# Splitting the levels of a WKV recurrence by feature halves and placing one batch's levels between the other's outputs

## The chip, the cores and the metric

The kernel runs on one core of one Trainium2 chip. The metric is the device time of one execution in microseconds; a smaller one is better. The kernel is one program that holds a whole small network (two layers of conditioning, token mixing, routing, attention and feed-forward). The change touches one stage of it, the recurrence of the first token mixer.

## The reference, cut to what matters

The stage computes the recurrence of an RWKV-6 mixer. For each of 2 batches there are 1024 tokens and 256 features in 4 heads of 64. `r`, `k`, `v` are projections of the tokens, `w` a decay between 0 and 1 for each token and feature, `u` a bonus for the token itself.

```
def step(S, inputs):                      # S: 64 x 64 for each head
    rt, kt, vt, wt = inputs
    kv = kt[..., :, None] * vt[..., None, :]
    y = jnp.einsum('bhi,bhij->bhj', rt, S + u[None, :, :, None] * kv)
    S = wt[..., :, None] * S + kv
    return (S, y)
...
mean = y.mean(-1, keepdims=True)
var = y.var(-1, keepdims=True)
yn = ((y - mean) * jax.lax.rsqrt(var + LN_EPS)).reshape(b, t, c)
yn = yn * ln_w + ln_b
return yn @ W_o
```

The result is added to the residual `x`. What follows (`cond2_0`, a gelu projection) needs the finished `x`.

## The kernel before, in words

Features lie on the partitions: 256 features are two halves `c` of 128 partitions, and each half holds two heads (`par`, 64 partitions each). `r[b]`, `kk[b]`, `w[b]` are tiles of 128 x 2 x 1024 for each batch `b`. Tokens are cut into 8 chunks (`ck`) of 128, and each chunk into two halves of 64.

The function `wkv` (line 399) never steps through tokens. It builds the triangular matrix A of all pairs (earlier token, later token) inside a chunk by levels:

- `diagonal` (427) makes the products of a token with itself, from `ru` = u times r (line 581, ScalarE), and places them on A's diagonal (443, VectorE).
- `level` (445) for l = 0 to 5, with h = 2^l: 64 matmuls of 64x64 by 64x32 for each batch and level (line 455) make the products of pairs that fall on two sides of a boundary of blocks of h tokens. They go to two PSUM banks, one for each `par`; both feature halves `c` lie in each bank. A matmul in fp32 leaves two records, so the profile counts 128 for a batch and level. VectorE copies the wanted entries to A under a mask for l up to 3 (468, two copies of 128x512), ScalarE for l = 4 and 5 (475, small blocks).
- `decay` (477) after each level multiplies k by the total decay behind it (483, GpSimd, 128x1024) and r by that before it (484, VectorE, 128x1024), in place, so that the next level can use them; line 486 then halves the table of total decays `tot`.
- `last` (489) makes the products between the two halves of a chunk (495, 64 records a batch), copied by ScalarE and VectorE (503), and a last decay.

Then `states` (506) transposes k (513, TensorE; 516, ScalarE copies to `kt`), makes each chunk's contribution to the state (530, copied to `pd` by 537) and runs a scan over the chunks (540, VectorE). `output` (543) makes two chunks of y at a time: products with A (552) and with the state (563) in two banks, which 574 (ScalarE) and 575 (VectorE) add into `y`. `tmix_out` (610) normalises 512 tokens and projects them: squares (618, ScalarE), sums (623), root (180 to 182), widened (628), transposed (634), multiplied (637, 638), and projected by `wo` (643) onto `x` (644).

The order of the work is set by the program text and by a planner that merges the engines' queues by its own cost table; the order of each queue is then fixed. Before the change the two batches alternate: for each level, batch 0's and then batch 1's (lines 583 to 586), with four banks named `sc` shared in turn. After both have passed all levels, `states` of both follow, then the four `output` steps of batch 0 and the four of batch 1, and between these the pieces of `tmix_out` for the 512-token chunks that are ready (lines 594 to 607). Tiles of the level part (`ru`, the tables `tot`) and of the output part (`kt`, `td`, `pd`, `st`) lie in two pools, one opened after the other.

SP's queue issues the loads of the next stage: `b2` (949), `c2w1`, `c2w2` and their small companions (134 to 144), then `w1c` (1068) and the first expert's weights (933, 935). Each waits until the memory that it is to fill is free, and each stands behind the ones before it.

Of the kernel before, what the change touches and what calls it, by code (L numbers as in the profile page):

```python
# [9 lines left out]
F32 = mybir.dt.float32  # L10
# [3 lines left out]
ALU = mybir.AluOpType  # L14
# [5 lines left out]
B = 2  # L20
# [378 lines left out]
def wkv(k, r, kk, w, v, y, x):  # L399

# [6 lines left out]
    with (  # L411
        tiles(tc, name="wka", bufs=1) as ap,
        tiles(tc, name="wkq", bufs=1, space=PSUM) as qp,
    ):
# [3 lines left out]

        A = [ap.tile([P, 2, 2, NC, P], F32, name=f"A{b}") for b in range(B)]
        tot = [w[b].rearrange("p c t -> p (c t)") for b in range(B)]  # L420
# [3 lines left out]
        def bank(pp, shape):  # L424
            return pp.tile(shape, F32, name="sc", bufs=4)

        def diagonal(pp, b, ru):

            for c in range(2):
                ps = [bank(pp, [P, NC, H]) for par in range(2)]  # L430
                for ck in range(NC):
                    for half in range(2):
                        ts = slice(ck * P + half * H, ck * P + (half + 1) * H)
                        for par in range(2):
                            nc.tensor.matmul(
                                ps[par][halves[half], ck, :],
                                lhsT=kk[b][halves[par], c, ts],
                                rhs=ru[halves[par], c, ts],
                                start=True,
                                stop=True,  # L440
                            )
                for par in range(2):
                    nc.vector.tensor_mul(A[b][:, par, c, :, 0:H], ps[par], eye.unsqueeze(1).to_broadcast([P, NC, H]))

        def level(pp, b, l):

            h = 1 << l
            ps = [bank(pp, [P, 2, NC, H // 2]) for par in range(2)]
            for c in range(2):
                for ck in range(NC):  # L450
                    for half in range(2):
                        ts = slice(ck * P + half * H, ck * P + (half + 1) * H)
                        for par in range(2):
                            rv = r[b][halves[par], c, ts].rearrange("p (n two h) -> p n two h", two=2, h=h)
                            nc.tensor.matmul(
                                ps[par][halves[half], c, ck, :],
                                lhsT=kk[b][halves[par], c, ts],
                                rhs=rv[:, :, 1, :],
                                start=True,
                                stop=True,  # L460
                            )
            for par in range(2):
                dv = A[b][:, par, :, :, 0:H].rearrange("p c n t -> p (c n) t")
                dv = dv.rearrange("p g (n two h) -> p g n two h", two=2, h=h)[:, :, :, 1, :]
                pv = ps[par].rearrange("p c n t -> p (c n) t").rearrange("p g (n h) -> p g n h", h=h)
                if h < 16:
                    m = k.lvl[:, l].rearrange("p g (n h) -> p g n h", h=h)
                    nc.vector.copy_predicated(dv, m, pv)
                    continue

                for s0 in range(0, P, 32):
                    n = (s0 % H) // (2 * h)
                    if s0 % (2 * h) < h:
                        ss = slice(s0, s0 + min(h, 32))
                        nc.scalar.copy(dv[ss, :, n, :], pv[ss, :, n, :])

        def decay(sp, b, l):
            h = 1 << l
            n = 2 * S // (2 * h)
            t2 = tot[b].rearrange("p (n two) -> p n two", two=2)  # L480
            kv = kk[b].rearrange("p c (n two h) -> p (c n) two h", two=2, h=h)
            rv = r[b].rearrange("p c (n two h) -> p (c n) two h", two=2, h=h)
            nc.gpsimd.tensor_mul(kv[:, :, 0, :], kv[:, :, 0, :], t2[:, :, 1].unsqueeze(2).to_broadcast([P, n, h]))
            nc.vector.tensor_mul(rv[:, :, 1, :], rv[:, :, 1, :], t2[:, :, 0].unsqueeze(2).to_broadcast([P, n, h]))
            nt = sp.tile([P, n], F32, name=f"tot{l}", bufs=2)
            nc.vector.tensor_mul(nt, t2[:, :, 0], t2[:, :, 1])
            tot[b] = nt

        def last(pp, b):

            for c in range(2):
                ps = [bank(pp, [P, NC, H]) for par in range(2)]
                for ck in range(NC):
                    for par in range(2):
                        nc.tensor.matmul(
                            ps[par][halves[0], ck, :],
                            lhsT=kk[b][halves[par], c, ck * P : ck * P + H],
                            rhs=r[b][halves[par], c, ck * P + H : (ck + 1) * P],
                            start=True,
                            stop=True,  # L500
                        )
                for par, copy in enumerate((nc.scalar.copy, nc.vector.tensor_copy)):
                    copy(A[b][halves[0], par, c, :, H:P], ps[par][halves[0]])
            decay(ap, b, 6)

        def states(sp, b):
            kt = sp.tile([P, NC, C], F32, name="kt", bufs=1)
            for n in range(0, M, 2):
# [7 lines left out]
                nc.scalar.copy(kt[:, n:e, :], pk[:, 0 : e - n, :])  # L516

            td = sp.tile([P, 2, H, M], F32, name="td")
# [5 lines left out]
            pd = sp.tile([P, 2, H, M], F32, name="pd", bufs=1)  # L524
# [13 lines left out]
            st = sp.tile([P, 2, H, M], F32, name="st")  # L538
            flat = [t.rearrange("p c j n -> p (c j n)") for t in (st, td, pd)]
            nc.vector.tensor_tensor_scan(flat[0], flat[1], flat[2], 0.0, ALU.mult, ALU.add)  # L540
            return st

        def output(sp, b, st, n):

            py = [qp.tile([P, 2, 2, 2, H], F32, name=f"py{half}") for half in range(2)]
            for c in range(2):
                for i in range(2):
# [12 lines left out]
                    for own in range(2 if ck else 0):  # L560
                        for half, hs in enumerate(halves):
# [3 lines left out]
                                lhsT=st[hs, c, :, ck - 1],  # L565
# [4 lines left out]
                            )  # L570
            yv = y[:, :, b * S + n * P : b * S + (n + 2) * P].rearrange("p c (i a t) -> p c i a t", i=2, a=2)
            for a in range(2):
                t = sp.tile([P, 2, 2, H], F32, name="half")
                nc.scalar.copy(t, py[0][:, :, :, a])
                nc.vector.tensor_add(yv[:, :, :, a], t, py[1][:, :, :, 1 - a])

        with tiles(tc, name="wks", bufs=2) as sp, tiles(tc, name="wkp", bufs=1, space=PSUM) as pp:
            for b in range(B):
                ru = sp.tile([P, 2, S], F32, name="ru")
                for c in range(2):  # L580
                    nc.scalar.activation(ru[:, c, :], r[b][:, c, :], AF.Copy, scale=k.vec("u", c))
                diagonal(pp, b, ru)
            for l in range(6):
                for b in range(B):
                    level(pp, b, l)
                    decay(sp, b, l)
            for b in range(B):
                last(pp, b)
        with (
            tiles(tc, name="wkt", bufs=2) as sp,  # L590
            tiles(tc, name="gos", bufs=1) as gs,
            tiles(tc, name="gop", bufs=1, space=PSUM) as gp,
        ):
            outs = [tmix_out(k, gs, gp, y, x, ch) for ch in range(NCK)]
            before = [states(sp, b) for b in range(B)]
            left = []
            for b in range(B):
                for n in range(0, NC, 2):
                    output(sp, b, before[b], n)
                    for _ in range(2):  # L600
                        if left and next(left[0], 1):
                            left.pop(0)
                    if n % 4 == 2:
                        left.append(outs[(b * S + n * P) // CK])
            for steps in left:
                for _ in steps:
                    pass


def tmix_out(k, sp, pp, y, x, ch):  # L610

# [28 lines left out]
    for c in range(2):  # L640
        po = pp.tile([P, CK], F32, name="pw", bufs=2)
# [976 lines left out]
def attn1_heads(k, b, x, ci, kT, v, sv, masks, rp, sp, pp, yp):  # L1618
# [22 lines left out]
    def behind(ins, other):  # L1641

        how = mybir.DependencyInfo(mybir.DependencyClass.NoSync, mybir.DependencyReason.DATA)
        k.tc.add_manual_dep(ins.ins, other.ins.name, how, reason="order")

# [75 lines left out]
    def exps(it, pair):  # L1721

        for view in window(it["at"][0]):
# [5 lines left out]
            if pair and it["no"]:  # L1729
                behind(e, rows["turned"])  # L1730
# [8 lines left out]
    def invert(it):  # L1739

        rd = sp.tile([P, 4], F32, name="rd")
        behind(nc.vector.reciprocal(rd, it["den"]), rows["least"])
        it["rdw"] = sp.tile([P, 4, 64], F32, name="rdw")
        behind(nc.scalar.copy(it["rdw"], rd.unsqueeze(2).to_broadcast([P, 4, 64])), rows["exp"])

    def turn(it):
# [25 lines left out]
        behind(masked, rows["least"])  # L1772
# [352 lines left out]
```

## Time and profile before

| what | value |
|---|---|
| median of 3 runs | 1491.24 us (1489.38 to 1491.75) |
| the profiled execution, its own time | 1490.23 us |
| its span in the profile | 1488.5 us (so 1.7 us lie around the span) |
| TensorE / VectorE / ScalarE / GpSimd busy over the span | 94% / 59% / 44% / 15% |
| last projection of the stage ahead ends, about | 132.5 us from the span's start |
| first diagonal matmul (435) | 134.21 us |
| first level matmul (455) to last (455) | 139.7 to 186.0 us |
| first transpose of the states (513) | 194.29 us |
| first matmul of the next stage, `cond2_0` (671) | 271.33 us |

So the stage takes the stretch from about 134 to 271 us, a tenth of the span. The profile's page gives averages over the whole span; what counts here is read from this stretch, with the view that gives each engine's busy time by stretches, and the view of instructions in order of time. In the first, each row has the stretch, its length, for each engine the busy time and the number of instructions (x), the clock granted to TensorE as a share of full speed, the share of the DMA engines and what they moved. In the second, a row has the start, the time, the engine, the line, operation and operands, the number of instructions merged, and in brackets how long the engine had been idle and what released it.

### The profile page before, as it was taken

Reading aid. Unit: us, or ns where it says so; the run is one execution under the profiler, and the core shown is the slowest. Engines: PE = TensorE matmul, PEld = TensorE weight load, DVE = VectorE, ACT = ScalarE, POOL = GpSimd, SP = SyncE. Lnnn points to the kernel's source line nnn. Section 1 sums busy time; section 2 is a strip of 40 time slices with the busy share of each in tenths; the row PEclk is TensorE's granted clock in tenths of the full one; section 3 lists DMA queues with packets and bytes.
Section 4 is the critical chain, followed back from the end, with each engine's and each line's share of the span. In section 5 each row is a group of like instructions: output and inputs, shape, how many; then the busy total and the mean of one; then the engine's idle time right before and its main releaser. Section 6 shows DMA issues by size and latency. Waiting matters only on the chain. (4 is left out here: it accounts for less than half of the span.)

```text
span 1488.5 us, 27374 instructions
## 1 busy us (share of the span) xinstructions
PE 1405.7 (94%) x10852; PEld 930.2 (62%) x10852; DVE 874.3 (59%) x2640; ACT 651.8 (44%) x1509; POOL 217.9 (15%) x201
## 2 busy tenths in 40 slices
PE   6998889999799999979999999999999999999998
PEld 3445877455556676656666644777776457777766
DVE  5545734121389942047787773577676637777674
ACT  3333242222222213207788832656564436556633
POOL 3333630022401632110000010000000200000011
PEclk9899678999889999989999999999999999999999
DMA  9600004300144343030000020000000000000001
GB/s 300 203 1 2 4 2 142 142 31 30 64 133 160 106 147 121 15 127 1 2 1 2 2 85 0 1 2 2 1 2 2 0 0 2 2 2 2 1 15 45
DMA packets 42759, 70.79 MB, mean 48 GB/s; under 512 B 7168, under 2 KB 35840, under 8 KB 39552
## 3 DMA queue, kind: packets, MB, share of 16 engines
q1 hardware_dynamic: 36576, 57.12, 11.4%
q0 software_dynamic: 3072, 8.65, 1.6%
q10 hardware_dynamic: 2976, 3.18, 0.7%
q8 instruction: 88, 1.44, 0.4%
q14 instruction: 47, 0.39, 0.1%
HBM read 45.09 MB, written 23.86 MB: 46 GB/s over the span
## 5 line engine op out<-in xcount | busy, mean ns | idle before, releaser
L1726 ACT ACTIVATE pe<-pe,nm 128x321 f32<-128x321 f32 x256 | 142.2, 559 | 109.2 <-DVE nm L1707 109.2
L1707 DVE CUSTOM_DVE_ANT_0 pe<-ps,wbs 128x321 f32<-128x321 f32 x256 | 114.8, 491 | 18.3 <-PE ps L1680 8.3
L1255 ACT ACTIVATE pe<-pe,nm 128x256 f32<-128x256 f32 x256 | 110.5, 498 | 19.6 <-DVE nm L1245 19.6
L988 PE MATMUL ph<-xt,w 128*128 128x512 f32 x256 | 114.3, 604 | 2.2 <-ACT xt L983 2.2
L996 PE MATMUL po<-w,h 128*128 128x256 f32 x512 | 111.8, 379 | 0.0
L996 PEld LDWEIGHTS po<-w,h 128*128 128x128 f32 x512 | 97.3, 190 | 16.6 <-issue 3.8
L1245 DVE CUSTOM_DVE_ANT_0 pe<-ps,lc 128x256 f32<-128x256 f32 x256 | 94.1, 417 | 19.1 <-PE ps L1229 18.2
L1680 PE MATMUL ps<-kT,qT 64*64 64x386 f32 (+3 forms) x1024 | 101.6, 490 | 3.2 <-ACT qT L1660 2.5
L918 DVE SCALAR_TENSOR_TENSOR lc<-iok,idx,lc 128x256 f32<-128x256 f32 x248 | 100.6, 500 | 0.0
L1810 PE MATMUL py<-ptt,v 128*64 128x128 f32 x1408 | 91.0, 277 | 0.0
L1000 POOL DMA_INDIRECT ys<-ye,row x32 | 63.0, 1970 | 180.4 <-DVE ye L999 160.7
L988 PEld LDWEIGHTS ph<-xt,w 128*128 128x128 f32 x256 | 48.6, 193 | 62.5 <-issue 55.9
L1810 PEld LDWEIGHTS py<-ptt,v 128*64 128x64 f32 x1408 | 75.5, 137 | 10.7 <-issue 10.7
L1757 PE MATMUL pt<-ident,pe 128*128 128x128 f32 x512 | 77.4, 280 | 0.0
L1264 PE MATMUL ptp<-ident,pe 128*128 128x128 f32 x512 | 73.0, 280 | 3.7 <-DVE pt L1268 3.0
L1264 PEld LDWEIGHTS ptp<-ident,pe 128*128 128x128 f32 x512 | 55.3, 141 | 30.9 <-ACT pe L1255 14.8
L991 ACT ACTIVATE h<-ph,vecs 128x512 f32<-128x512 f32 x64 | 44.0, 687 | 69.5 <-PE ph L988 69.5
L1757 PEld LDWEIGHTS pt<-ident,pe 128*128 128x128 f32 x512 | 56.8, 141 | 12.5 <-issue 10.0
L999 DVE TENSOR_TENSOR ye<-po,b 128x256 f32<-128x256 f32 x32 | 13.9, 434 | 79.2 <-PE po L996 79.2
L1680 PEld LDWEIGHTS ps<-kT,qT 64*64 64x64 f32 x1024 | 33.3, 132 | 42.1 <-issue 24.4
L1765 DVE TENSOR_TENSOR ptt<-pt,near 128x1024 f32<-128x1024 f32 x48 | 58.6, 1220 | 0.4 <-PE pt L1757 0.4
L671 PE MATMUL ph<-x,c2w 128*128 128x512 f32 (+2 forms) x160 | 58.4, 508 | 0.0
(365 smaller groups left out, 2674.3 us busy)
## 6 DMA issues: line engine op xcount, KB each, us to landing
w<-in_mw SPq DMA_DIRECT2D x16, 1024.0 KB, 5.0
xs<-z SPq DMA_DIRECT2D x8, 1088.0 KB, 12.0
ys<-z SPq DMA_DIRECT2D x4, 1024.0 KB, 11.3
xe<-xs SPq DMA_DIRECT2D x7, 544.0 KB, 7.2
more<-xs SPq DMA_DIRECT2D x7, 544.0 KB, 4.1
out_x<-o SPq DMA_DIRECT2D x8, 256.0 KB, 2.2
x<-in_xT SPq DMA_DIRECT2D x3, 512.0 KB, 6.3
wa<-in_wa SPq DMA_DIRECT2D x1, 1536.0 KB, 8.0
```

What stands on the lines that cost most here:

```text
L918: nc.vector.scalar_tensor_tensor(n, key, k.idx[:, qb, j : j + 1], n, ALU.is_equal, ALU.add)
L988: nc.tensor.matmul(ph, lhsT=w1[:, c, m * P : (m + 1) * P], rhs=xt[:, c, :], start=c == 0, stop=c == 1)
L996: nc.tensor.matmul(po, lhsT=h[:, m, j * P : (j + 1) * P], rhs=w2[:, m, :], start=m == 0, stop=m == 7)
L1000: nc.gpsimd.indirect_dma_start(out=rows[e * 4 + j], out_offset=bass.IndirectOffsetOnAxis(ap=row[:, j : j + 1], axis=0), in_=ye[:, j, :], i ...
L1245: nc.vector.tensor_tensor_reduce(out=pe[:, j, :], in0=it["ps"][i][:, j, :], in1=k.lc[:, q0 + j, :], scale=-1.0, scalar=3.0e38, op0=ALU.add ...
L1255: nc.scalar.activation(pe[:, j, :], pe[:, j, :], AF.Exp, bias=nm, scale=-1.0)
L1264: nc.tensor.transpose(ptp[:, kb, j, :], it["pe"][i][:, j, kb * P : (kb + 1) * P], k.ident)
L1680: nc.tensor.matmul(ps[hps[half], view.head, c0:c1], lhsT=rows["qT", n // 2, m // 4][hp, (m + pair) % 4, qs], rhs=kT[hp, m + pair, view.sta ...
L1707: rows["least"] = nc.vector.tensor_tensor_reduce(out=pe[:, j], in0=ps[:, i, view.used : view.used + W], in1=wbs[:, o : o + W], scale=-1.0, ...
L1726: e = nc.scalar.activation(part, part, AF.Exp, bias=it["nm"][:, col], scale=-1.0, accum_out=it["den"][:, col])
L1757: nc.tensor.transpose(to[:, 2 * pair + view.head, :], pe[:, at : at + P], k.ident)
L1810: nc.tensor.matmul(py[64 * i : 64 * i + 64, (m + pair) % 4, :], lhsT=keys[j][:, hs], rhs=it["pt"][:, j, 2 * pair + i, :], start=False, sto ...
```

## The change

- `level`, `decay` and `last` become one generator, `levels(b)`, that works by feature halves. For each level and each half c: 32 matmuls, then `decay(b, l, c)` on 128x512 (GpSimd and VectorE), then the copies of that half to A (VectorE 128x256, or ScalarE with half as long blocks). A manual order puts VectorE's copies behind its own decay. After the second half comes `total(b, l)`.
- The two banks of a level are still one for each `par` and hold both halves.
- Batch 0's levels run alone, with three pairs of banks in turn (`sc`, `py`, `pk`/`pu`). Batch 1's have the pair `sc` alone; one half level is taken at each step of batch 0's `states` and `output`, so they stand between the instructions of these.
- `states` of batch 1 comes after that, then the outputs of batch 1.
- Memory: `ru` is written into `y`, the tables `tot` into w and one tile T for each batch, `kt` and the states into w, `td` and `pd` into k. The pools of the output part are gone, and all is open from the start. The projections of `tmix_out` go to the banks `pk` and `pu`, which `states` uses too.

The core of the diff:

```
+        turns = [("sc0", "sc1"), ("py0", "py1"), ("pk", "pu")]
+        def banks(shape):
+            turns.append(turns.pop(0))
+            return [qp.tile(shape, F32, name=n) for n in turns[-1]]
...
+        def decay(b, l, c):
             h = 1 << l
+            n = S // (2 * h)
+            t2 = tot[b].rearrange("p (c n two) -> p c n two", c=2, two=2)[:, c]
+            kv = kk[b][:, c].rearrange("p (n two h) -> p n two h", two=2, h=h)
+            rv = r[b][:, c].rearrange("p (n two h) -> p n two h", two=2, h=h)
+            nc.gpsimd.tensor_mul(kv[:, :, 0, :], kv[:, :, 0, :], t2[:, :, 1].unsqueeze(2).to_broadcast([P, n, h]))
+            return nc.vector.tensor_mul(
+                rv[:, :, 1, :], rv[:, :, 1, :], t2[:, :, 0].unsqueeze(2).to_broadcast([P, n, h])
+            )
...
+        def levels(b):
+            for l in range(6):
+                h = 1 << l
+                ps = banks([P, 2, NC, H // 2])
+                for c in range(2):
+                    for ck in range(NC):
+                        for half in range(2):
...
+                    scaled = decay(b, l, c)
+                    for par in range(2):
+                        dv = A[b][:, par, c, :, 0:H]
...
+                        if h < 16:
+                            m = k.lvl[:, l, 0:NC].rearrange("p g (n h) -> p g n h", h=h)
+                            behind(k, nc.vector.copy_predicated(dv, m, pv), scaled)
+                            continue
...
+                                nc.scalar.copy(dv[ss, :, n, :], pv[ss, :, n, :])
+                    if c:
+                        total(b, l)
+                    yield
...
+        for b in range(B):
+            diagonal(b)
+        for _ in levels(0):
+            pass
+        turns[:] = [("sc0", "sc1")]
+        beside = levels(1)
+        for _ in outputs(0):
+            next(beside, None)
+        for _ in beside:
+            pass
+        for _ in outputs(1):
+            pass
...
-        po = pp.tile([P, CK], F32, name="pw", bufs=2)
+    for c, name in enumerate(("pk", "pu")):
+        po = pp.tile([P, CK], F32, name=name)
```

`outputs(b)` is a new generator: `states(b)` (which now yields after each transposed pair of chunks and after each half of the contributions), then the four `output` steps, each with a yield in its middle and at its end, and after each up to two pieces of `tmix_out`.

In the built program every other stage has the same instructions in the same order on all five queues; one load, `w1ak` (1513), moves from the end of the row of loads to its front.

## The prediction

> **What bounds the stage now.** The page's chain of work that ended last says nothing here: followed back, it ends in the attention. So I read the stretch from 134 to 271 us in two views. First, busy time by stretches: diagonal, levels 0 to 3, levels 4 and 5, `last`, states, outputs, and the last chunk's tail up to the next stage's first matmul (271.33).
>
> ```profile
> 134.20:140.20 6.00, 5.16 (x258) 4.64 (x258) 4.77 (x15) 3.08 (x3) 0.00 (x0) 1.00 0.01 3
> 140.20:174.90 34.70, 28.09 (x1160) 27.26 (x1163) 30.85 (x27) 0.00 (x0) 19.14 (x8) 0.69 0.02 4
> 174.90:186.20 11.30, 9.13 (x390) 8.77 (x384) 3.68 (x3) 8.10 (x20) 8.81 (x3) 0.73 0.02 5
> 186.20:194.30 8.10, 6.88 (x131) 6.42 (x127) 4.47 (x6) 4.47 (x8) 6.46 (x3) 0.60 0.02 4
> 194.30:212.40 18.10, 15.53 (x192) 11.36 (x192) 5.99 (x7) 6.55 (x14) 4.93 (x3) 0.78 0.00 1
> 212.40:259.90 47.50, 46.72 (x532) 37.23 (x530) 18.23 (x37) 15.08 (x29) 2.86 (x12) 0.83 0.33 107
> 259.90:271.30 11.40, 9.03 (x33) 5.52 (x32) 3.76 (x6) 3.00 (x4) 0.00 (x0) 0.70 0.62 243
> ```
>
> The reader is to see that levels 0 to 3 are VectorE's (third engine column: 30.85 of 34.70 us, with 27 instructions that follow each other), that the outputs are TensorE's (46.72 of 47.50), and that VectorE has 29 us free in the outputs. That is what the change is after: VectorE's work of one batch beside TensorE's work of the other.
>
> Second, the order in time, for the prices:
>
> ```profile
> 140.26 2.06 PE L455 MATMUL sc<-r,k 64*64 64x32 f32 x125 [0.30 <-DVE A L443]
> 142.36 2.51 DVE L468 COPY_PREDICATED A<-lvls,sc 128x512 f32<-128x512 uint8 x2 [0.96 <-PE sc L455]
> ...
> 158.95 1.32 DVE L468 COPY_PREDICATED A<-lvls,sc 128x512 f32<-128x512 uint8 x2 [0.21 <-PE sc L455]
> 159.26 2.11 POOL L483 TENSOR_TENSOR k<-k,tot 128x1024 f32<-128x1024 f32 x1 [1.61 <-PE sc L455]
> 160.18 2.28 DVE L484 TENSOR_TENSOR r<-r,tot 128x1024 f32<-128x1024 f32 x1
> ...
> 175.00 1.23 DVE L484 TENSOR_TENSOR r<-r,tot 128x1024 f32<-128x1024 f32 x1 [1.02 <-PE sc L455]
> 175.10 2.95 POOL L483 TENSOR_TENSOR k<-k,tot 128x1024 f32<-128x1024 f32 x1 [2.20 <-PE sc L455]
> ```
>
> A decay of r that starts before GpSimd's takes 1.23 us and GpSimd's then 2.95; one that starts later takes 2.28. One waits for the other. And TensorE's clock:
>
> ```profile
> 151.00:154.00 3.00, 2.96 (x111) 2.86 (x106) 2.95 (x4) 0.00 (x0) 2.41 (x1) 0.50 0.02 5
> 166.00:169.00 3.00, 2.18 (x128) 2.07 (x127) 2.48 (x4) 0.00 (x0) 2.03 (x1) 1.00 0.03 5
> ```
>
> At the granted clock 0.50 a level's record takes 2.96/111 = 26.7 ns, at 1.00 2.18/128 = 17.0 ns. A half level has 64 records: 1.71 or 1.09 us.
>
> **The wait that the halves bring.** Both halves lie in the same two banks. In the built program the second half's matmuls wait for VectorE's (ScalarE's, at l = 4 and 5) copies of the first half: 18 of the 64 records for the first copy, 46 for the second. So within a level nothing of the second half runs beside the copies of the first; what TensorE does run ahead is the next level's first half, in another pair of banks. Batch 1 has one pair alone, so there every half level waits for the copies of the one before it. The handover from copy to copy is: 0.05 us from VectorE to TensorE (the copy before the 140.26 row ended at 140.2), 46 records (1.23 us at clock 0.50, 0.78 at 1.00), and 0.2 us to VectorE's start (diagonal: started at 134.21, 64th record at 135.25, VectorE at 135.43). That is 1.5 or 1.0 us. I take 1.5: in 147 to 164 us the clock stood at 0.50, and there a level's 128 records came every 3.7 us; the new stage brings fewer (below).
> The Trainium skill speaks against this sharing: "PSUM — Partial Sum Buffer", section "PSUM bank collisions raise a hardware error", says to guard the PSUM by bank and 32-partition quadrant, not by address, so halves in one bank cannot overlap on two engines. No row here shows a matmul into a bank that is being read; by addresses alone the sum would be that of the third rival.
>
> **Part 1: batch 0's levels alone.** VectorE's prices for a half: decay 0.68 (the table's halving of 128x512, line 486, took 0.684); two copies 2 x 0.65 at l = 0 and 1 (half of 2.51, with a little start-up), 2 x 0.38 at l = 2 and 3 (half of 1.32). Unknown is what GpSimd's half decay costs VectorE: nothing if VectorE is first, half of 2.28 - 1.23 = 0.5 if last; I take 0.5 for the first halves at l = 2 and 3, where the row shows it, and keep 0 and 0.5 everywhere as ends.
> - Start: VectorE is free of the diagonal at 140.9 (before, 141.4: the halvings of `tot` that stood between its copies move into the handovers, which hide them: 0.68, 0.42 and 0.28 us in the first).
> - l = 0, 1: 2 x (2 x (0.68 + 1.3) + 1.5) = 10.9. l = 2, 3: 2 x (2 x (0.68 + 0.76) + 0.5 + 1.5) = 9.8. To 161.6.
> - l = 4, 5: ScalarE's copies took 0.361 (256 elements) and 0.576 (512), so 0.25 for 128: 8 a half, 2.0, then 4 x 0.36 = 1.45. 2 x 2.0 + 1.3 + 2 x 1.45 + 1.3 = 9.5, pick-up 0.5. To 171.6.
> - `last`: 92 records took 5.19 us at clock 0.5, so 32 take 1.8; then GpSimd's half decay, 3.46/2 = 1.7. The states' transposes can begin at 171.6 + 1.8 + 0.2 + 1.7 = **175.3**. Before, at 194.29. Gain 19.0 us: batch 1's levels are gone from here, but batch 0's take 34 us alone where both took 54.
>
> **Part 2: batch 1's levels between batch 0's states and outputs.** Twelve half levels in series: 4 x (1.5 + 1.98) = 13.9; 4 x (1.5 + 1.44) = 11.8; 2 x (1.3 + 2.0) = 6.6; 2 x (1.3 + 1.45) = 5.5; the two groups of `last` with their copies (0.58) 2 x 2.1 = 4.2. Sum 42.0. What the states and outputs put into these queues: on VectorE the scan (2.03, half of it beside a group's matmuls: 1.0), the copy to `td` (0.85) and y's adds (0.42 each), mostly in handovers: 0.8. On TensorE about 8 instructions stand between two half levels; 128 records of an output step took 3.25 us (216.62 to 219.86), so 0.4 us, hidden beside copies of 0.76 to 1.3 us. Together 43.8: to **219.1**. Done by then: batch 0's states, three of its four outputs, and the sums (623) of chunk 0.
>
> **Part 3: the rest.** Before, seven outputs and `tmix_out` of chunks 0 to 2 took 47.5 us. Now: two outputs fewer (3.55 and 3.25 us in the trace, so -6.8), chunk 0's sums gone (-1.95), batch 1's states more (transposes 5.7 and contributions 6.8 us of TensorE for both batches, so +6.25), and 0.5 for their banks, shared with the projection (643), whose add (644, 0.69) must read them first. 45.5: to 264.6. The tail of the last chunk stays, 11.4: **276.0**, against 271.3.
>
> The loads do not stand in the way. `c2w1` was issued at 226.90; now it waits for batch 1's scan, by the sum near 243, and lands in 6.4 us, needed at 276. `c2w2` of batch 1 waits for the last output, some 15 us ahead of the next stage, as `w1c` did (256.37); it is used only with that stage's third chunk. The loads behind them on SP's queue, the experts', were issued at 257 to 272 and are first used at 415.6. If this cover were gone, a load costs its 5 to 7 us. `ru` in `y`'s place costs nothing: what read that memory was the zero fill, whose traffic ended by 74 us (the page's GB/s row); nor does `w1ak`, issued behind that fill into an idle queue.
>
> **Sum.** +4.7 us on the profiled execution, 1490.23: 1494.9. The median shown is 1.0 above it; I write **1495**. A difference under 0.2% (3 us) cannot be told from none.
>
> **Rivals.**
> 1. The clock stays up (ends faster). All 18 handovers were priced at clock 0.50, six in part 1 and twelve in part 2, and so were the four groups of `last`. At 1.00: 18 x 0.45 + 4 x 0.55 = -10.3, so 1484.5. For it: each queue of matmuls is short of 2 us of pause, and at 164 and 181 us the clock came back with VectorE still the pace. Against: it fell at 147 after one pause of 1.7 us and stayed down 17 us though TensorE is recorded busy 2.96 of 3.00. It decides from a mean clock of about 0.8 between 141 and 219 us: above that the change is no longer slower.
>    The Trainium skill, "TensorE: Matmul & The Clock Gate", section "HAM oscillation — how this bites in real kernels", gives the rule that only idle gaps over about 3.4 us lower the clock; by it the sum would be this rival's. The trace's fall after 1.7 us differs.
> 2. The fill holds up the levels (slower still). TensorE's queue is in order: where an output or state instruction between two half levels waits itself (for `kt`'s copy, 0.59, or the two of y's half, 0.65), batch 1's next group stands behind it. At 0.6 us for each of 13 gaps, +7.8: 1503. For it: in 194 to 212 the transposes waited 2.5 us in all for `kt`. Against: most gaps hold products with A, which wait for nothing.
> 3. The halves overlap after all, and the handovers of the second halves are hidden: 12 x 1.5 = -18, 1477. The built program's waits speak against it.
> That the change doesn't reorder as said is out: the built order shows batch 1's half levels between batch 0's instructions.
>
> **Chances.** Forecast 0.50 (its own range 1491 to 1500: GpSimd's 0.5 us at 0 and everywhere is -1 and +4), rival 1 0.27, rival 2 0.18, rival 3 0.05. Range 1482 to 1505: it takes in rivals 1 and 2 and leaves out the third and the outer ends. Faster by over 0.2% (under 1488.3): most of rival 1 (0.23) and rival 3, 0.28. Within: the rest of rival 1 and the low end of the forecast (0.14), 0.18. Slower (over 1494.2): 0.54.
>
> **What would show it.** In the profile after: the first transpose of the states near 175; VectorE idle some 1.5 us before each second half's decay, released by TensorE; batch 1's last level group near 217; 45 us from there to the last chunk's sums; the clock near 0.5 to 0.7 in the levels. The prediction is wrong in part 1 if VectorE shows no such pauses, in part 2 if the twelve half levels take under 36 or over 50 us, in part 3 if the next stage starts more than 60 us after the last of them, or waits for a load.

## The result, and the profile after

The changed kernel takes **1515.9 us** (median of 5 runs, 1513.7 to 1518.1) against 1489.4 us before (5 runs beside them, 1488.4 to 1491.8): ratio 1.0173, 95% interval 1.0159 to 1.0188. It is slower, as forecast, but by 26.5 us and not by 5: outside the range. The profiled execution took 1515.1 us, its span is 1513.3.

The change renumbers lines: level matmul 455 -> 488; VectorE's copy 468 -> 502, ScalarE's 475 -> 509; decay 483 -> 463 (GpSimd) and 484 -> 464 (VectorE); halving 486 -> 474; last 495 -> 517; transposes 513 -> 540; outputs 552 and 563 -> 579 and 590; sums 623 -> 650.

First, busy time by stretches of the changed kernel: levels 0 to 3 of batch 0, its levels 4 and 5, its last group, batch 1's levels between states and outputs, the rest, the tail. The columns are those of the first table of the prediction.

```profile
137.50:164.60 27.10, 17.75 (x521) 17.12 (x514) 15.99 (x30) 0.04 (x1) 12.42 (x8) 0.55 0.01 3
164.60:176.70 12.10, 9.65 (x226) 9.39 (x226) 2.97 (x5) 7.14 (x25) 6.35 (x5) 0.50 0.01 3
176.70:179.10 2.40, 2.10 (x58) 2.00 (x59) 1.95 (x4) 0.99 (x2) 2.05 (x2) 0.75 0.00 0
179.10:235.00 55.90, 52.26 (x1057) 48.28 (x1057) 25.34 (x46) 15.08 (x40) 22.70 (x15) 0.58 0.01 3
235.00:281.50 46.50, 44.97 (x464) 34.15 (x465) 17.70 (x35) 14.86 (x29) 5.15 (x14) 0.84 0.22 71
281.50:292.80 11.30, 8.93 (x35) 5.39 (x34) 4.43 (x7) 3.00 (x4) 0.00 (x0) 0.85 0.78 273
```

The reader is to see three things. VectorE, which set the pace of levels 0 to 3 before (30.85 of 34.70 us), is now busy 15.99 of 27.10: it waits. The fourth row is 55.9 us long where 43.8 were predicted, at clock 0.58. The last two rows are as predicted (45.5 and 11.4). The next stage's first matmul comes at 292.85, not at 271.33.

Second, the order in time, VectorE in the levels 2 and 3 of batch 0:

```profile
151.70 0.72 DVE L464 TENSOR_TENSOR r<-r,w 128x512 f32<-128x512 f32 x1
152.34 0.75 DVE L502 COPY_PREDICATED A<-lvls,sc 128x256 f32<-128x256 uint8 x2
156.76 0.69 DVE L464 TENSOR_TENSOR r<-r,w 128x512 f32<-128x512 f32 x1 [3.68 <-PE sc L488]
...
163.30 0.69 DVE L464 TENSOR_TENSOR r<-r,w 128x512 f32<-128x512 f32 x1 [3.63 <-PE py L488]
```

VectorE's work on a half is as priced (0.69 and 0.75). What is not is the bracket: before a second half's decay it waits 3.6 us for TensorE. The forecast said 1.5. (In levels 0 and 1 the bracket is 1.53 and 1.73, but there VectorE halves `tot` meanwhile: from the end of its copies to the decay it is 3.2 and 2.2 us.) How the 3.63 us ahead of 163.30 pass is shown by three more rows of the order in time: VectorE's copies of the first half of level 3, and TensorE behind them.

```profile
158.93 0.74 DVE L502 COPY_PREDICATED A<-lvls,py 128x256 f32<-128x256 uint8 x2
160.01 0.31 PE L488 MATMUL pk<-r,k 64*64 64x32 f32 x1 [2.04 <-POOL k L463]
160.59 2.54 PE L488 MATMUL py<-r,k 64*64 64x32 f32 x61
```

`py` is what everybody waits for, level 3's second half. It could begin when the copies end, at 159.67. But `pk`, level 4's first half, stands ahead of it in TensorE's queue, where the planner put it, and that needs GpSimd's decay of level 3's first half: it starts at 160.01 (0.34 us). Its nine matmuls take until 160.47 (0.46). Then `py`'s 64 records start between 160.47 and 162.95 (2.48 us, 38.7 ns each and not 26.7), and VectorE starts 0.35 later. The clock is 0.50 all that time. The view of line 488 has the idle time of TensorE by what ended it:

```profile
  POOL k L463: 18.8, 9
...
  DVE A L502: 1.9, 2
```

GpSimd is named nine times for 18.8 us. Most of that would have been a wait for the copies anyhow; the view names the one that came last, here by 0.34 us.

### The profile page after: what moved, and what is told of

It reads as the page before. It is cut to its first block, busy times and chain, and to the rows that moved or that the text cites. A ratio compares the mean times of both kernels' runs of the same rounds, so it can differ in the third digit from the quotient of the medians.

```text
span 1513.3 us, 27478 instructions
## 1 busy us (share of the span) xinstructions
PE 1424.8 (94%) x10852; PEld 949.6 (63%) x10852; DVE 874.3 (58%) x2670; ACT 656.1 (43%) x1533; POOL 195.9 (13%) x215
## 3 DMA queue, kind: packets, MB, share of 16 engines
q1 hardware_dynamic: 36576, 57.12, 11.3%
## 5 line engine op out<-in xcount | busy, mean ns | idle before, releaser
L1015 PE MATMUL ph<-xt,w 128*128 128x512 f32 x256 | 113.7, 602 | 2.2 <-ACT xt L1010 2.2
L1272 DVE CUSTOM_DVE_ANT_0 pe<-ps,lc 128x256 f32<-128x256 f32 x256 | 94.2, 417 | 18.8 <-PE ps L1256 18.7
L1779 PEld LDWEIGHTS pt<-ident,pe 128*128 128x128 f32 x512 | 56.8, 141 | 12.5 <-issue 10.0
L1027 POOL DMA_INDIRECT ys<-ye,row x32 | 34.4, 1076 | 208.1 <-DVE ye L1026 187.7
L1702 PEld LDWEIGHTS ps<-kT,qT 64*64 64x64 f32 x1024 | 33.3, 132 | 42.2 <-issue 23.8
## 6 DMA issues: line engine op xcount, KB each, us to landing
xs<-z SPq DMA_DIRECT2D x8, 1088.0 KB, 11.3
```

The source lines that it names most:

```text
L1015: nc.tensor.matmul(ph, lhsT=w1[:, c, m * P : (m + 1) * P], rhs=xt[:, c, :], start=c == 0, stop=c == 1)
L1272: nc.vector.tensor_tensor_reduce(out=pe[:, j, :], in0=it["ps"][i][:, j, :], in1=k.lc[:, q0 + j, :], scale=-1.0, scalar=3.0e38, op0=ALU.add ...
L1702: nc.tensor.matmul(ps[hps[half], view.head, c0:c1], lhsT=rows["qT", n // 2, m // 4][hp, (m + pair) % 4, qs], rhs=kT[hp, m + pair, view.sta ...
L1779: nc.tensor.transpose(to[:, 2 * pair + view.head, :], pe[:, at : at + P], k.ident)
```

## The experiments

The stage is measured in the traces, since the stages ahead vary: the first diagonal matmul came between 131.2 and 136.1 us in kernels whose code ahead of it is the same. **Part 1** is from the diagonal's end to the states' first transpose, **part 2** from there to batch 1's last level group, **the rest** to the next stage's first matmul; **all** is from the first diagonal matmul.

| kernel | time, us | part 1 | part 2 | rest | all |
|---|---|---|---|---|---|
| before | 1489.4 | 52.9 (both batches) | | 77.0 | 137.1 |
| after | 1515.9 | 41.7 | 55.9 | 57.9 | 161.7 |
| after, again (e8) | 1526.9 | 42.2 | 57.8 | 61.5 | 167.9 |
| e1_banks | 1504.4 | 28.0 | 57.3 | 59.9 | 151.3 |
| e2_order | 1503.1 | 37.1 | 53.9 | 50.7 | 148.3 |
| e2_order again (e9) | 1499.3 | 37.1 | 52.6 | 48.4 | 144.3 |
| e2b_inner | 1504.2 | 39.2 | 52.2 | 53.3 | 151.0 |
| e2c_groups | 1517.5 | 39.2 | 56.8 | 60.4 | 162.5 |
| e5_warm | 1509.7 | 41.5 | 48.1 | 55.8 | 151.5 |
| e7_warm_order | 1496.6 | 36.2 | 49.8 | 52.5 | 144.6 |
| e3_order_banks | 1489.0 | 27.8 | 36.7 | 59.6 | 130.4 |
| e3_order_banks again (e6) | 1484.2 | 28.1 | 37.7 | 59.3 | 131.2 |
| e4_alternate | 1492.0 | 53.1 (both) | | 74.6 | 133.8 |
| e4b_alt_order | 1490.8 | 52.2 (both) | | 75.6 | 133.9 |

Times other than those of before, after and e6 are single ones; the kernel before, beside them, took 1492.5 (e1, e2, e2b, e2c), 1486.0 (e3, e4, e4b, e5) and 1489.4 (e8, e9); beside e6 and e7 its median was 1489.9 (17 runs, 1477.9 to 1492.1). So single times can be off by several us, and two traces of one kernel differ by 0.8 to 6.3 us in the stage. How much filling work falls into part 2 differs, so part 2 and the rest are best read as a sum.

**A pair of banks for each half of batch 0.**

```
-                ps = banks([P, 2, NC, H // 2])
+                ps = None
                 for c in range(2):
+                    ps = ps if c and b else banks([P, 2, NC, H // 2])
```

> Batch 0's two halves of a level get a pair of banks each, three pairs in turn; batch 1 keeps its one pair. In the changed kernel the stretch from the diagonal's end (137.5 us) to the states' first transpose (179.1) took 41.6 us, and the stretch from there to batch 1's last level group 55.8. Theory A (the shared banks force the second half to wait for the copies of the first, and what the wait costs is set by the order of TensorE's queue behind it): without sharing there is nothing to wait for, VectorE and GpSimd run through. By VectorE's rows that is 8 x (0.69 + 1.3) or (0.69 + 0.75) = 13.7 for levels 0 to 3, by GpSimd's 1.6 to 1.75 a half some 20 for all six levels, then ScalarE's 6.9 for the levels 4 and 5 and 4 for the last groups: 26 to 30 us instead of 41.6, 12 to 15 off the time, so 1500 to 1503 us. Theory B (the pace is GpSimd's half decay, which costs almost as much as a whole one, with or without sharing): 36 us or more, 1510 and over. Theory C (TensorE at half its clock is the pace): 64 records of 38.7 ns for each of 12 halves, 30 us, and the last groups: 35 us, 1509. In all three the second stretch stays at 55 to 57 us.

Part 1 fell to 28.0 us, as the theory of the shared banks said, and the time by 12, to 1504.4 where 1500 to 1503 was expected. VectorE hardly waits any more:

```profile
152.06 0.69 DVE L464 TENSOR_TENSOR r<-r,w 128x512 f32<-128x512 f32 x1 [0.22 <-PE py L489]
```

GpSimd's half decays (20.4 us busy of 28.0) and the clock (0.57 in this stretch, 0.55 in the changed kernel's) can't have been the pace, as theories B and C would have it with 35 us or more. But removing the sharing removed the planner's odd order too: in the built program batch 0's matmuls now stand in the order of the text. So this run alone doesn't tell the wait from the order.

**The order of TensorE's queue, whole and in its two halves.** Banks shared as in the changed kernel.

```
+                                m = nc.tensor.matmul(
...
+                                ahead[b] = behind(k, m, ahead[b]) if ahead[b] else m
```

> The level matmuls of a batch keep the order of the program text on TensorE's queue, across halves and levels; banks are shared as in the changed kernel. So no matmul of the next level's first half stands before or among those of the second half, and the matmuls alternate between the two banks and the two halves of the chunk. Theory A (the planner's order of TensorE's queue made the handover 2.2 to 3.7 us instead of the 1.5 that was predicted: it put matmuls that wait for GpSimd's decay ahead, and several in a row on the same quarter of the array): the handovers fall to 1.5 to 1.9 us, the first stretch from 41.6 to 34 to 37 us, the second from 55.8 to 44 to 50, and the time to 1497 to 1506 us. Theory B (GpSimd's half decays are the pace): first stretch 40 us or more, 1512 to 1517. Theory C (the wait for the bank costs a whole group of 64 records at half the clock, whatever the order): 6 x 2.5 us stay, both stretches within 2 us of the changed kernel's, 1512 to 1517.

> One half of the edit of the order: within a group of 32 matmuls (one level, one half of the features) TensorE's queue keeps the order of the text, but the next level's first half may still be put among the matmuls of the current second half, and it is, from its first nine on. If it is the nine of the next level that wait for GpSimd's decay which cost the time, the handovers stay at 3.5 us in the levels 1 to 3 of batch 0 and the first stretch at 39 to 42 us; the second stretch, where no other pair of banks is free and so nothing of the next level can run ahead, is the place where the order within a group shows alone: 46 to 52 us instead of 55.8 if it is worth 0.4 to 0.8 us for each of 12 handovers, 55 to 57 if not. So 1506 to 1514 us by the first, 1513 to 1517 by the second.

> The other half of the edit of the order: a group may begin only behind the whole group before it, so nothing of the next level runs ahead of the current second half; within a group the planner's order stays, nine matmuls of one bank first. If the look-ahead that waits for GpSimd is the cost, the first stretch falls from 41.6 to 35 to 38 us and the second stays at 54 to 57: 1508 to 1513 us. If the order within a group is the cost, the first stretch stays over 39 us and the time is 1512 to 1517. If neither is, both stay.

The waits before the second half's decay in level 2 (e2_order, then e2c_groups):

```profile
155.44 0.69 DVE L464 TENSOR_TENSOR r<-r,w 128x512 f32<-128x512 f32 x1 [2.04 <-PE sc L490]
```

```profile
156.34 0.69 DVE L464 TENSOR_TENSOR r<-r,w 128x512 f32<-128x512 f32 x1 [2.43 <-PE sc L491]
```

In e2b_inner they are 3.46 in level 2 and 3.40 in level 3. So of the 3.65 us what runs ahead is worth 1.2 (3.65 - 2.43), the order within the group 0.4 (2.43 - 2.04), and 2.04 is left in the order of the text. Part 1 lost 2.5 us by either half of the edit and 4.6 by both; no single one of the expectations for the halves holds, they share it. (In e2b_inner 1.5 of the 2.5 came in levels 4 and 5.) The whole order gave less than theory A expected of it: handovers of 2.04 and not 1.5 to 1.9, part 1 of 37.1 and not 34 to 37, part 2 of 53.9 and not 44 to 50; the time, 1503.1, is inside its range. In e2_order GpSimd's decay no longer ends any idle time of TensorE ahead of a level matmul; VectorE's copies do, 12 times, a microsecond each:

```profile
  DVE A L505: 12.6, 12
```

What was not foreseen is where most of the gain arose. Part 2 and the rest fell from 113.7 to 104.6 us in e2_order and 105.5 in e2b_inner, but not in e2c_groups (117.2). The clock differs: in the changed kernel and in e2c_groups it stood at 0.50 from 188 and 181 us to 242, in e2_order and e2b_inner it came back at 200.5 and 201.6.

**Is that chance?** Both kernels were profiled again.

> The changed kernel again, for a second trace. If the clock's course in the second stretch (0.50 from 188.1 to 242.7 us) belongs to the order of the work, it is there again, and the stretch from the first diagonal matmul to the next stage's first is 159 to 164 us, as 161.7 was. If it is chance, the clock comes up earlier in this trace and the stretch is 150 to 157, and the gains that e2_order, e2b_inner and e5_warm showed there prove nothing.

> e2_order again, for a second trace. If the order of the text brings the clock back near 200 us, as it did there (148.3 us from the first diagonal matmul to the next stage's first), the stretch is 146 to 152 us and the clock over 0.9 somewhere between 200 and 214. If that was chance, the stretch is 156 us or more, with the clock at 0.50 from 188 to 240.

It is not: both traces of e2_order (148.3 and 144.3 us for the stage) are at least 13 us shorter than both of the changed kernel (161.7 and 167.9). e9's clock changed within 0.2 us of e2's at 142, 176, 187, 200 and 214 us, and its stage is a little under the expected 146 to 152. The changed kernel stayed down in the levels again, this time without any break from 145.1 to 250.9 us, and took 167.9 us for the stage, the longest of all and above the expected 159 to 164. So the changed kernel's clock did not take the same course twice, and the size of the gain is uncertain by some 6 us. Its row for that stretch, with TensorE busy 92.7 of 104 us:

```profile
146.00:250.00 104.00, 92.66 (x1904) 86.51 (x1902) 45.09 (x83) 24.04 (x67) 43.74 (x28) 0.50 0.01 2
```

**The clock by itself.** The order of batch 0's work untouched, one unused full-size matmul behind each of batch 1's half levels 0 to 3:

```
+                    if b and l < 4:
+                        pn = qp.tile([P, 2, C], F32, name="nb")
+                        behind(k, nc.tensor.matmul(pn, lhsT=k.ident, rhs=v[:, 0:2, :], start=True, stop=True), m)
```

> The changed kernel with one more matmul of 128x128 by 128x512, whose result nothing uses, behind each of batch 1's half levels 0 to 3 (8 in all); it stands in TensorE's queue where the next group waits for copies. Such a matmul keeps TensorE some 0.8 us at full clock by the rows of the next stage (0.41 us a record, two records), 1.7 at half. Batch 0's levels are untouched: first stretch 40 to 42 us. Theory C (the clock at 0.50 from 188 to 236 us is what makes the second stretch long: groups of 2.2 to 2.6 us instead of 1.1 to 1.3): if the extra matmuls keep the clock over 0.8 there, the second stretch falls from 55.8 to 44 to 50 us and the time to 1500 to 1508. If the clock stays at 0.5, the matmuls only add, up to 8 x 1.3 us: second stretch 57 to 66, 1516 to 1526. Theory A (the waits for copies, not the clock): clock up, stretch unchanged, 1513 to 1517.

The clock came up, and with eight matmuls more part 2 became 7.8 us shorter, the whole stage 10.2. (The time, 1509.7, is 1.7 above the expected range; the stage began 5 us later than in the changed kernel's trace, behind the same code.) First the changed kernel, then this one, 212 to 224 us in the table by stretches, and a group of one half level in each:

```profile
212.00:224.00 12.00, 11.52 (x242) 11.02 (x240) 2.83 (x5) 6.85 (x22) 4.14 (x4) 0.50 0.01 3
```

```profile
223.76 2.67 PE L488 MATMUL sc<-r,k 64*64 64x32 f32 x62
```

```profile
212.00:224.00 12.00, 11.26 (x341) 9.87 (x335) 3.68 (x8) 4.97 (x19) 4.66 (x4) 0.93 0.01 3
```

```profile
212.79 1.50 PE L488 MATMUL sc<-r,k 64*64 64x32 f32 x62
```

341 records instead of 242 in the same 12 us. A TensorE that is recorded busy 11.5 of 12 us is not one that does its most.

> e2_order with one unused matmul of 128x128 by 128x512 behind each half level 0 to 3 of both batches (16 in all). In e2_order the clock stood at 0.50 from 142.5 to 176.7 us and VectorE waited 2.04 us for each second half of the levels 1 to 3 of batch 0. Theory C (the handover is 64 records at the granted clock): if the clock comes up in the first stretch, the waits fall to 1.2 to 1.5 us (64 records of 17 ns and 0.3), the first stretch from 37.1 to 32 to 35 us; if it stays at 0.50 although TensorE has more to do there, the waits are 2.0 to 2.6 and the stretch 37 to 42. In the second and third, where e2_order's clock was up about half of the time, 0 to 4 us less than its 104.6 if the clock stays up, and up to 8 more if not. Time 1494 to 1503 by the first, 1503 to 1515 by the second.

Here the clock was up in part 1 too (0.86), and the waits of VectorE are the shortest with shared banks:

```profile
155.70 0.69 DVE L464 TENSOR_TENSOR r<-r,w 128x512 f32<-128x512 f32 x1 [1.24 <-PE sc L490]
```

So in the order of the text the handover is 64 records at the granted clock and 0.3 us: 2.04 at 0.50 (26.7 ns a record), 1.24 at 1.00 (14.6). Part 1 gained only 0.9 us of it, short of the 32 to 35 expected: the first halves of levels 2 to 4 came later, behind the unused matmuls (VectorE waited 1.8, 0.8 and 0.8 us for them; 0 to 0.4 in e2_order). The stage, 144.6, is no shorter than e9's, 144.3.

**Is it the batch that runs alone?** Half levels, shared banks, but the batches alternate as before the change:

```
+        for _ in zip(levels(0), levels(1)):
             pass
...
```

> Half levels as in the changed kernel, banks shared by the two halves, planner's order, but batch 1's half level follows batch 0's, with three pairs of banks in turn for both, then the states of both, then the outputs, as before the change. So each batch's wait for its banks stands beside the other's copies. If running one batch alone is what made the halves expensive, the levels take VectorE's 27.4 us for levels 0 to 3 of both batches and ScalarE's 14 for levels 4 and 5, the first transpose comes at 188 to 194 us (194.3 before the change), and the time is 1484 to 1493 us. If the halves cost by themselves (GpSimd's 28 half decays of 1.6 to 1.75 us, 46 us, and the order of TensorE's queue), the first transpose comes after 197 and the time is 1496 us or more.

> As e4_alternate, with the level matmuls of both batches in the order of the text on TensorE's queue. If the planner's order costs in the alternation too, 2 to 6 us under e4_alternate; if the other batch's work covers it, within 2 us of it.

With the other batch beside it, the handover is covered: 53.1 us for all levels against 52.9 with whole levels before. The first transpose, at 195.0, lies between the two expected ranges, since the stage began 1.6 us later than before; the time is inside the first. Halves are no gain there either: VectorE is busy 42.8 instead of 37.8 us and GpSimd 40.4 instead of 34.4, since two half decays take longer than a whole one (by the medians 2 x 0.69 for 1.32 on VectorE, 2 x 1.51 for 2.66 on GpSimd). The order is worth 0.9 us at most here. So the halves hurt where one batch alone must hide its own handover. The stage as a whole is 3.2 to 3.3 us shorter than before in both runs, 1 us of it in the diagonal and most of it behind the levels; no run says what that comes from, and the two single times don't show it.

**Order and banks together**, with `nv` and `nb` as a second pair for batch 1:

```
-                ps = banks([P, 2, NC, H // 2])
                 for c in range(2):
+                    ps = banks([P, NC, H // 2])
...
-        turns[:] = [("sc0", "sc1")]
+        turns[:] = [("sc0", "sc1"), ("nv", "nb")]
```

> Order of the text on TensorE's queue as in e2_order, and a pair of banks for each half level: three pairs in turn for batch 0, two (the second is nv and nb) for batch 1. First stretch (diagonal's end to first transpose): 27 to 29 us, as e1_banks had 28.0 with the banks alone. Second stretch (to batch 1's last level group): theory A (the halves wait for the copies in their shared banks) gives VectorE's or ScalarE's pace, 33 to 42 us instead of 53.9 in e2_order, and the time 1484 to 1495 us. Theory C (at clock 0.50 TensorE's own work is the pace there: in the changed kernel it was busy 52.3 of 55.9 us) gives 48 us or more where the profile shows the clock near 0.5, and 1498 to 1503 us.

> e3_order_banks once more, timed in five rounds against the kernel before the change. In its profile the stretch from the first diagonal matmul to the next stage's first matmul was 130.4 us, against 137.1 before the change and 161.7 after it; but its one time was 3.0 us above the one of the kernel before beside it. If the stage is what counts, and the 3 us came from the stages around it, it is faster than before by up to 6.7 us: 1482 to 1489 us where the kernel before has 1486 to 1492, ratio 0.995 to 1.000. If the stretch in that one profile was a lucky course of the clock, the ratio is 1.000 to 1.003.

```profile
139.00:167.10 28.10, 23.31 (x809) 22.30 (x801) 22.48 (x38) 8.17 (x26) 20.55 (x14) 0.57 0.02 4
167.10:204.80 37.70, 27.44 (x998) 24.94 (x1000) 28.07 (x44) 13.08 (x37) 21.60 (x15) 0.91 0.02 4
```

With the order of the text in both, banks of their own take part 1 from 37.1 us (e2_order) to 27.8 and 28.1, at mean clocks of 0.54 and 0.57; the order alone had taken it from 41.7 to 37.1. So of part 1's 13.9 us the sharing is 9.3 and the order of the queue 4.6. These two rows of e6_repeat stand against the first four of the changed kernel: 65.8 us instead of 97.5 for the same levels. The clock was up in the second (0.91), so what the banks and what the clock did there is not told apart. The version is faster than both kernels, though by 0.26% only against the one before: 1484.2 us (12 runs, 1479.4 to 1488.9) against 1489.9 (17 runs), ratio 0.9974, interval 0.9954 to 0.9994. The stage's 6 us were there in both traces.

## Why the prediction was wrong, step by step

- **The step that failed is "The handover from copy to copy ... I take 1.5"**, and every sum that uses it. It took "46 records (1.23 us at clock 0.50 ...)". The count of 46 was right for the planner's order, the 26.7 ns for an even one; no kernel here had both. In the order of the text (e2_order) the matmuls alternate between the two banks, so nearly all 64 records wait for the second copy: 64 x 26.7 ns + 0.34 = 2.05, measured 2.04. In the planner's order nine matmuls of one bank stand ahead of nine of the other, and records that follow each other on one bank came 53 ns apart (e2c_groups, 153.72 to 154.35 us, against 26.7 from 155.02 to 155.66, where the banks alternate): the group took 2.26 us from first to last start, the wait was 2.43. And "what TensorE does run ahead is the next level's first half" was seen and costed at nothing, while those matmuls came in front of the second half: 0.34 us for GpSimd, 0.46 for themselves, then all 64 records at 38.7 ns, the 18 of the first bank too, and 0.35 to VectorE's start: 3.63.
- **Part 1**: predicted 34.4 us from VectorE's first free moment to the transposes, measured 41.3 (137.8 to 179.1). By VectorE's decays: levels 0 and 1 took 13.9 us for 10.9, levels 2 and 3 12.9 for 9.8, levels 4 and 5 12.1 for 9.5 and 0.5, the last group 2.4 for 3.7. The start came 3.1 us earlier than written, for the stage ahead ended earlier in this execution; the point 175.3 so looks nearer to 179.1 than its sum was. That is luck. With the order of the text it is 10.25 for the 9.8 of levels 2 and 3.
- **Part 2**: predicted 43.8, measured 55.9. The twelve half levels, from the first decay (181.5) to the last group's (230.1), took 48.7 us; the prediction's 13.9 + 11.8 + 6.6 + 5.5 and 1.8 of others' work on the queues make 39.6. VectorE's waits in levels 2 and 3 were 2.2 to 2.3, not 1.5. It named the bound: "if the twelve half levels take under 36 or over 50 us"; 48.7 is just inside, the two ends (2.4 and 4.9) made the rest. The clock, put at 0.5 throughout, was 0.58: here the assumption held, and the size of a group at that clock (2.1 to 2.9 us from first to last start of 64 records instead of 1.7) did not: here nothing of a next level runs ahead, so it is the planner's order within the group and the two or three instructions of states and outputs inside it, which no run separates. With the clock up the same halves took 40.5 us (e5_warm, 186.0 to 226.5).
- **Part 3 and the tail**: 45.5 and 11.4, measured 46.5 and 11.3. Outputs, states, sums and projections were moved as costed, and no load stood in the way.
- **GpSimd**: half decays took 1.49 to 1.75 us, one 2.03 (1.7 was written for level 6). The cost to VectorE when GpSimd is first was under-sized: 2.02 and 1.99 instead of 0.69, so 1.3 and not 0.5, but only in level 0 of each batch at that size.
- **Rivals**: the clock did not stay up by itself; what it is worth in part 2 and the rest is shown by e5_warm, 9.8 us with the eight matmuls' own time in it; the rival had priced it at 10.3 for parts 1 and 2. The fill hardly delayed the start of batch 1's groups: in part 2 they begin 0.04 to 0.26 us behind the copy that frees their first bank, not 0.6 at 13 gaps. The overlap of the halves, rival 3, needs banks of their own: e3_order_banks is that kernel, and its two traces are 31.3 and 30.5 us below the changed one in the stage.
- **Order of size.** For part 2, the rest and the tail the prediction had 43.8 + 45.5 + 11.4 = 100.7 us; the changed kernel took 113.7, e2_order 104.6 and 101.0 in its two traces. So with the order of the text, and the clock that came with it, that sum holds within 4 us, and part 1 within 2.4 (36.8 for 34.4): most of the miss went with the order of TensorE's queue. The stage is 24.6 us longer than before. By e1_banks 10.4 of it are the sharing in part 1 alone (order included); by e3_order_banks sharing and order in both parts are all of it and 6 more.

## What to carry to other kernels

Splitting a step into halves brings overlap only if the halves don't share what is handed over; count what waits for the last release in the built order, not in the text, and price what runs ahead by its own time and waits, since in an in-order queue all that stands behind it pays them. A step that loses its neighbour loses the cover of its handovers: beside the other batch the same halves took no longer than whole levels. And before one of two queues is filled with small matmuls, ask at which clock they will run.

## What the runs showed of the hardware that was not expected

The granted clock changed only after whole multiples of 3.41 us (11 of them, 37.5 us, and 16, 54.6 us, in the changed kernel; 31, 105.8 us, in its second trace), and it stayed at 0.50 all that time though TensorE's recorded pauses there were at most 2.75 us in part 1 and 0.53 in part 2. The Trainium skill, "TensorE: Matmul & The Clock Gate", section "What's actually happening", says that full clock comes after about one busy window of 3.4 us; by the recorded busy time of these traces that should have ended it many times, and the traces decide. What the recorded busy time leaves out is how much of TensorE's array a matmul fills. Compare two windows of 3.41 us at clock 0.50, the first of the changed kernel, the second of e5_warm; both are busy throughout, and only behind the second, which has fewer records but the two of an unused full-size matmul among them, did the clock rise:

```profile
205.19:208.60 3.41, 3.41 (x94) 3.41 (x93) 1.37 (x3) 0.00 (x0) 1.55 (x1) 0.50 0.02 5
```

```profile
193.12:196.53 3.41, 3.41 (x53) 2.21 (x50) 1.98 (x4) 0.00 (x0) 1.74 (x1) 0.50 0.02 5
```

Count each record by rows x columns of the array x columns of its result, a level's record (64x64 by 64x32) as 1, so that a record of 128x128 by 128x512 is 64. By the records that start in them these two windows have 139 and 184. In all whole windows that begin between 130 and 295 us, in all fourteen traces: at clock 0.50 it rose behind 1 of 140 windows with under 110 and behind 22 of 22 with 200 or more; at 1.00 it fell behind 48 of 48 with under 110 and behind none of 242 with 180 or more. Between these it did both. A level's records at clock 0.50 make at most 128 in a window (26.7 ns each), so alone they stay where it mostly remained down (it rose behind 15 of 104 windows of 100 to 130); one full-size matmul adds 128. These counts were made from the traces afterwards, and no run was made to test them. Whether matmuls into a bank that is being read would overlap stays open: every kernel here waited.
